# Attention probabilities read back through GpSimd's DMA queue, an activation table load tied to a later place, and extra TensorE products ahead of the first real ones

## The chip, the cores and the metric

The kernel runs on one core of a Trainium2 chip. The metric is the device time of one execution in microseconds (us). The kernel before takes 2250.06 us (median of three runs, 2249.04 to 2250.57). A profile of one execution shows what each engine did: TensorE (PE, with its weight loads as PEld), VectorE (DVE), ScalarE (ACT), GpSimd (POOL) and SyncE (SP), which issues most of the transfers between SBUF, the memory on the core, and DRAM.

## The reference

Four sequences of 512 tokens with 512 channels pass through two layers. Each layer has an attention-like part and a feed-forward part, each behind a gate made from a second input f:

```python
x = x + mamba2(bi_wkv(x, f, f, ...))          # layer 0, scan
x = x + moe(bi_wkv(x, f, f, ...))             # layer 0, 8 experts, top 2
x = x + grouped_attention(bi_wkv(x, f, f, ...))   # layer 1, 16 heads in 4 groups
x = x + silu_ffn(bi_wkv(x, f, f, ...))        # layer 1, 1408 wide
```

The gate runs two exponential averages over time, forward and backward, over `exp(k)*v` and `exp(k)`, and gives `sigmoid(r) * num / den`. Of the attention, these lines matter here:

```python
scores = einsum('bqgpd,bkgd->bgqpk', q, k) * SCALE
scores = where(causal, scores, -inf)
probs  = softmax(scores, axis=-1)
ctx    = einsum('bgqpk,bkgd->bqgpd', probs, v)
out    = einsum('bse,eh->bsh', ctx, w_dense)
```

## The kernel before, in words

Activations are held with channels on the 128 partitions and time along the free axis; weights stand still in TensorE's array and activations stream through it, 512 columns at a time. All products are in 32-bit floating point, except for the last stage, which splits its activations in two. The program is written as one stream. A planner that builds it sets the order of the instructions on each engine from the dependencies and from its own estimate of their costs. `tc.issue_after(i)` forces what is issued inside it to come behind `i` on the same engine; `after(engine)` does so for the last instruction that the engine has been given, and `Tables.use` ties a load of ScalarE's function table behind all activations that used the table before. Each engine carries out its instructions strictly in its own order, and a transfer queue sends off its transfers in order too: one that waits for data or for a free buffer holds those behind it.

**The opening (L943 to L1331).** The gate of sequence 0 is made in two pairs of channel blocks by `gate_pair` (L221): scans on VectorE, exponentials on ScalarE. L322 writes `den` times its reciprocal, L326 and L331 finish the gate, and L1311 multiplies it with the activated input into `first`, the input `h` of the scan stage. The weights `wxb` are loaded from L963 on. Eight PSUM banks (`ahead`, L1304) are taken in advance. `conv_products` (L1050, products at L1052) fills them with half of the sum after the first pair and the other half after the second; `conv_taps` (L1060, L1067) applies the four-tap convolution on VectorE. `time_steps` (L971, products at L977) needs a bank of the kind `tp`, two of which are among those eight, so it waits until the taps of one of them are done. `pump` fetches steps of the next gates' work, which VectorE does in between.

**Attention (L1568 to L1805).** There are 64 heads, in an outer order of group, sequence, and four heads within both. For a group and sequence `start_group` makes keys (`pk`, L1609) and values (`pv`, L1617). For a head `queries` makes `pq` (L1631) one head ahead, `scores` makes four query blocks of 128, 256, 384 and 512 keys (`psc`, L1653), masks them (L1656), takes the negated maximum (L1658), the exponential with its sum on ScalarE (L128, by way of L1663), divides by the sum (L1665), and turns blocks of 32x32 on VectorE into the SBUF tile `turned` (L1669), of which there are two. The other half of the transposition is done by memory: GpSimd issues four transfers that write `turned` to DRAM (L1677), and SP issues one that reads it back as `pT` (L1694, in `collect`), of which there are two buffers. `collect(1)` stands at the start of the next head's scores and leaves the youngest head in DRAM. `context` (L1719) multiplies `pT` with the values three heads later, and after each fourth head `dense` (L1734) applies the output weights and adds to the residual (L1742). The last two heads are transposed by TensorE (L1706). `nudge` (L1660) lets VectorE do a step of the gates of layer 1 between a maximum and the exponentials; those gates load `kt`, `ek` and `ekv` on SP's queue (L240, L247, L249). At the end of the stage `act.use(act.SILU)` (L1805) loads the table that the feed-forward stage needs.

Of the kernel before, what the change touches and what calls it, by code (L numbers as in the profile page):

```python
# [18 lines left out]
P = 128  # L19
B, T, C = 4, 512, 512  # L20
NC = C // P
# [62 lines left out]
def block_kernel(ctx: ExitStack, tc: tile.TileContext, a: dict, out: bass.AP):  # L84
    nc = tc.nc

    @contextmanager
    def after(*engines):

        with ExitStack() as es:  # L90
            for e in engines:
                last = next(
                    (i for i in reversed(nc.cur_bb.bb.instructions) if i.engine == e.engine), None
                )
                if last is not None:
                    es.enter_context(tc.issue_after(last))
            yield
# [35 lines left out]
    act = Tables()  # L133
# [32 lines left out]
    ident = const.tile([P, P], F32, name="ident")  # L166
# [51 lines left out]
    eks = [dr.tile([P, NC, T], F32, name=f"ek{b}") for b in range(B)]  # L218
    ekvs = [dr.tile([P, NC, T], F32, name=f"ekv{b}") for b in range(B)]

    def gate_pair(l, b, c0, dst=None, tiles=None):  # L221


        many = {"kt": 2, "ek": 2, "num": 2, "ekv": 1 if l < 2 else 2}
# [72 lines left out]
        den = tile_("den", 2)  # L297
# [14 lines left out]
        if tiles is not None or l >= 2:  # L312
            yield True

        r = tile_("rec", 2)
# [6 lines left out]
        nc.vector.scalar_tensor_tensor(  # L322
            flat(den), flat(den), DEN_MIN, flat(r), ALU.max, ALU.mult
        )
        yield False
        nc.vector.scalar_tensor_tensor(  # L326
            flat(num), flat(num), tf_out[:, b : b + 1], flat(r), ALU.mult, ALU.mult
# [573 lines left out]
    with ExitStack() as ph:  # L901
# [13 lines left out]
        first = even.tile([P, NC, T], F32, tag="h", name="h0_0")  # L915
# [9 lines left out]
        def lend_halves():  # L925

            left = []
            def take():
# [6 lines left out]
        lent = [  # L935
            {"f": lend("y", 3), "eu": lend("tmp", 2)},
            {
                "kt": lend("zs", 3), "ek": lend_halves(), "ekv": lend("xde", 2),
                "f": lend("xdt", 2), "eu": lend("bc", 4), "den": lend("st", 1, (P, DI)),
                "rec": lambda: lend("yT", 1, (P, NDI, P))().rearrange("p (i t) -> p i t", t=T),  # L940
            },
        ]
        pairs = [gate_pair(0, 0, c0, first, lent[c0 // 2]) for c0 in range(0, NC, 2)]  # L943
        for pair in pairs:
            for _ in range(6):
                for _ in step(pair):
# [8 lines left out]
        wxb = wx.tile([P, NC, NX], F32, name="wxb")  # L955
# [339 lines left out]
        def rounds(n):  # L1295
# [8 lines left out]
        ahead = [(m % NCV, ps_) for m, ps_ in zip(  # L1304
            range(NDI, NDI + 8), [ps_mm] * 4 + [ps_acc] * 2 + [ps_tp] * 2)]
        ahead = [(m, ps_("pc")) for m, ps_ in ahead]
        for c0, pair in zip(range(0, NC, 2), pairs):
            for _ in pair:
                pass
            for cc in range(c0, c0 + 2):  # L1310
                nc.vector.scalar_tensor_tensor(  # L1311
                    first[:, cc, :], turned[cc], 1.0, first[:, cc, :], ALU.add, ALU.mult
                )
            for m, pc in ahead:
                conv_products(w.h, m, pc, range(c0, c0 + 2))
# [202 lines left out]
    with tc.tile_pool(name="moe_w2", bufs=1, reuse_waits="tile") as wm:  # L1518
# [33 lines left out]
        n = len(nc.cur_bb.bb.instructions)  # L1552
# [15 lines left out]
    with att as ph:  # L1568
# [120 lines left out]
        def collect(rest=0):  # L1689

            while len(away) > rest:
                d = away.pop(0)
                back[id(d)] = pT = new_pT()
                nc.sync.dma_start(  # L1694
                    out=pT.rearrange("p r k j -> p (r k j)"), in_=d.rearrange("c i r s -> (c i) (r s)")
                )

        def context(u, prs):

# [46 lines left out]
        def settle():  # L1746

            old, done = held.pop(0)
            context(old, done)
            if len(old.ctxT) == HPG:  # L1750
                dense(old)

        weights, dense_w = {0: first_group}, {0: load_dense(0)}
        heads_ = [(g, b, i) for g in range(GROUPS) for b in range(B) for i in range(HPG)]
# [21 lines left out]
        for n, (g, b, i) in enumerate(heads_):  # L1776
            u, qT = ready
            if g == 0 and i == 0 and b + 1 < B:
                combine(b + 1, (0, 1))
                look_ahead(b + 1, (2, 3))  # L1780
            if g == 0 and i == 1 and b + 1 < B:
                combine(b + 1, (2, 3))
            if g == 0 and i == 3 and b + 2 < B:
                look_ahead(b + 2, (0, 1))
            if g == 2 and i == 0 and b < 3:
                to, name = ((ffg_d, "gateT"), (ffu_d, "upT"), (ffd_d, "downT"))[b]
                nc.sync.dma_start(out=to, in_=a[name])
            if g and b == 0 and i == 3:
                dense_w[g] = load_dense(g)
            if n + 1 < len(heads_):  # L1790
                ready = begin(n + 1)
            if g == 0 and i == 2 and b + 1 < B:
                act.use(act.EXP)
                hs[b + 1] = gated(2, b + 1, x[b + 1], gp, tag="h", name=f"h2_{b + 1}")
                act.use(act.LOG_EXP)
            prs = scores(u, i, qT)
            held.append((u, prs))
            if len(held) > 3:
                settle()
        while held:  # L1800
            settle()
        for _ in making:
            pass
        send()
        act.use(act.SILU)  # L1805


    LOW = 0xFFF
# [2 lines left out]
    with ExitStack() as ph:  # L1811
# [48 lines left out]
        for lo, hi in ((0, 4), (4, 8), (8, NFF)):  # L1860
            nc.sync.dma_start(
                out=wdn[:, lo:hi, :],
                in_=ffd_d[lo * P : hi * P, :].rearrange("(i p) m -> p i m", p=P),
            )

        for b in range(B):
            hd = []
            for i in range(NFF):
                cs = slice(i * P, (i + 1) * P)
# [38 lines left out]
        with tc.If(n_odd > 0):  # L1908
            with ExitStack() as gen:
                wl = gen.enter_context(tc.tile_pool(name="ff_gen", bufs=2, **right))  # L1910
                for b in range(B):
                    h = gated(3, b, x[b], gp, tag="h", name=f"h4_{b}")
                    hd = []
                    for i in range(NFF):
                        cs = slice(i * P, (i + 1) * P)
                        pv = []
                        for name in ("gateT", "upT"):
                            w = wl.tile([P, NC, P], F32, tag=name, name=name)
                            nc.sync.dma_start(
                                out=w, in_=a[name][:, cs].rearrange("(k p) m -> p k m", p=P)  # L1920
# [13 lines left out]
                    for m in range(NC):  # L1934
                        w = wl.tile([P, NFF, P], F32, tag="downT", name="downT")
                        nc.sync.dma_start(
                            out=w,
# [77 lines left out]
```

## Time and profile before

| what | us |
|---|---|
| median of three runs | 2250.06 |
| profiled execution, its own time | 2257.3 |
| its span, first to last instruction | 2255.4 |
| start of TensorE's first long work (L1052) | 42.02 |
| start of attention's keys (L1609) | 1129.81 |
| last dense products of attention begin (L1734) | 1995.81 |

The span is a little shorter than the profiled execution's own time, which includes what lies around it. How attention's TensorE work looks late in the stage, when no gates are made any more (start, duration, engine, line, operation, tiles, records; a product in 32-bit floating point leaves two records):

```profile
1949.51 3.60 PE L1631 MATMUL pq<-h,wq 128*128 128x512 f32 x8
1952.95 2.32 PE L1653 MATMUL psc<-kT,qT 128*128 128x128 f32 x8
1955.11 2.32 PE L1719 MATMUL pctx<-pT,v 128*128 128x512 f32 x8
1957.26 3.60 PE L1631 MATMUL pq<-h,wq 128*128 128x512 f32 x8
1960.70 2.32 PE L1653 MATMUL psc<-kT,qT 128*128 128x128 f32 x8
1962.86 2.32 PE L1719 MATMUL pctx<-pT,v 128*128 128x512 f32 x8
1965.01 13.90 PE L1734 MATMUL pd<-cx,wd 128*128 128x512 f32 x32
```

One head follows another without a gap: queries of the next head, scores of this one, context of the head three before. Starts show the pace better than durations, since the modelled ends overlap a little with the next start.

### The profile page before, as it was taken

The numbers are of one execution on the slowest core, as the hardware profiler recorded it, in microseconds if no ns is written. First come the engines' busy times: TensorE is split into PE (matmuls) and PEld (weight loads), VectorE is DVE, ScalarE is ACT, GpSimd is POOL, SyncE is SP. The second block draws the span as 40 slices with busy tenths as digits, with TensorE's granted clock in tenths as the row PEclk, the third lists the DMA queues.
The fourth block names the chain that finished last, engine by engine and source line by source line (L and its number), as shares of the span: only waits on it lengthen the run. The fifth ranks groups of instructions, "written<-read, shape, count | busy, mean of one in ns | idle before, by whom it ended". The sixth has DMA issues, their size and how long they took to land. (4 is left out here: it accounts for less than half of the span.)

```text
span 2255.4 us, 23842 instructions
## 1 busy us (share of the span) xinstructions
PE 2133.1 (95%) x7528; PEld 1227.2 (54%) x7528; DVE 1523.8 (68%) x3040; ACT 969.9 (43%) x1898; POOL 418.5 (19%) x558
## 2 busy tenths in 40 slices
PE   2879999999999999999989999999999999999998
PEld 1445565565665444444445555555555555568887
DVE  8697989989753566576577777577767765465332
ACT  4475676675842233333154433333334332243221
POOL 4023232322222111222211111111111111100000
PEclk9888999999999999999989999999999999999999
DMA  7542251342433457988576555455545464441100
GB/s 263 169 145 66 89 173 66 110 157 76 139 119 126 145 201 274 366 298 301 205 253 196 187 173 176 137 170 177 173 153 169 141 194 136 145 156 38 38 19 20
DMA packets 112454, 357.38 MB, mean 158 GB/s; under 512 B 14594, under 2 KB 23170, under 8 KB 102914
## 3 DMA queue, kind: packets, MB, share of 16 engines
q1 hardware_dynamic: 87584, 277.26, 36.3%
q0 software_dynamic: 22432, 74.34, 10.9%
q10 hardware_dynamic: 2304, 4.20, 0.5%
q8 instruction: 62, 1.02, 0.2%
q14 instruction: 72, 0.57, 0.1%
HBM read 337.91 MB, written 108.00 MB: 198 GB/s over the span
## 5 line engine op out<-in xcount | busy, mean ns | idle before, releaser
L1677 POOL DMA_DIRECT2D turned<-turned x248 | 135.2, 552 | 697.2 <-DVE turned L1669 393.7
L1631 PE MATMUL pq<-h,wq 128*128 128x512 f32 x512 | 233.2, 597 | 1.1 <-DVE h L404 0.8
L1734 PE MATMUL pd<-cx,wd 128*128 128x512 f32 x512 | 224.1, 594 | 3.1 <-ACT cx L1727 2.8
L128 ACT ACTIVATE pr<-psc,nmax 128x128 f32<-128x128 f32 (+3 forms) x256 | 134.6, 526 | 166.8 <-DVE nmax L1658 163.7
L1052 PE MATMUL pc<-h,wxb 128*128 128x512 f32 x320 | 150.9, 628 | 43.6 <-DVE h L1311 38.6
L1656 DVE TENSOR_TENSOR psc<-psc,mask 128x128 f32<-128x128 f32 x256 | 70.7, 284 | 144.3 <-PE psc L1653 144.1
L1653 PE MATMUL psc<-kT,qT 128*128 128x128 f32 (+3 forms) x512 | 155.7, 440 | 9.5 <-ACT pr L128 9.1
L1719 PE MATMUL pctx<-pT,v 128*128 128x512 f32 (+3 forms) x512 | 152.9, 438 | 9.4 <-DMA pT<-turned 9.1
L1734 PEld LDWEIGHTS pd<-cx,wd 128*128 128x128 f32 x512 | 95.5, 190 | 120.0 <-issue 107.9
L1631 PEld LDWEIGHTS pq<-h,wq 128*128 128x128 f32 x512 | 93.5, 192 | 97.2 <-issue 90.7
L1719 PEld LDWEIGHTS pctx<-pT,v 128*128 128x128 f32 x512 | 97.1, 191 | 90.0 <-issue 60.2
L845 PE MATMUL po<-w,yT 128*128 128x512 f32 x296 | 134.2, 593 | 0.9 <-DMA w<-in_w2x 0.7
L812 PE MATMUL pg<-w,hT 128*128 128x512 f32 x296 | 134.3, 594 | 0.0
L823 PE MATMUL pn<-w,hT 128*128 128x512 f32 x296 | 133.4, 593 | 0.5 <-DMA w<-in_w1x 0.5
L1052 PEld LDWEIGHTS pc<-h,wxb 128*128 128x128 f32 x320 | 62.5, 201 | 116.7 <-issue 74.4
L1742 DVE TENSOR_TENSOR xr<-xr,pd 128x512 f32<-128x512 f32 x64 | 43.6, 681 | 120.5 <-PE pd L1734 120.5
L1658 DVE TENSOR_REDUCE nmax<-psc 128x1 f32<-128x128 f32 (+3 forms) x256 | 122.4, 482 | 2.0
L1669 DVE STREAM_TRANSPOSE turned<-pr 128x128 f32<-128x128 f32 x248 | 120.5, 498 | 1.8
L1653 PEld LDWEIGHTS psc<-kT,qT 128*128 128x128 f32 x512 | 85.1, 191 | 66.8 <-issue 26.1
L1271 PE MATMUL po<-wot,yT 128*128 128x512 f32 x256 | 115.0, 603 | 0.0
L1123 PE MATMUL pz<-wzt,h 128*128 128x512 f32 x256 | 114.6, 596 | 0.3 <-ACT st L1224 0.3
L1665 DVE TENSOR_SCALAR pr<-pr,rsum 128x128 f32<-128x128 f32 (+3 forms) x256 | 95.5, 374 | 1.7
(343 smaller groups left out, 4146.9 us busy)
## 6 DMA issues: line engine op xcount, KB each, us to landing
w<-in_w1x SPq DMA_DIRECT2D x76, 1024.0 KB
turned<-turned POOLq DMA_DIRECT2D x248, 208.0 KB, 4.0
pT<-turned SPq DMA_DIRECT2D x62, 832.0 KB
w<-in_w2x SPq DMA_DIRECT2D x38, 1024.0 KB
wb<-in_b1x SPq DMA_DIRECT2D x38, 512.0 KB
lm<-cs SPq DMA_DIRECT2D x32, 512.0 KB
kt<-in_fT SPq DMA_DIRECT2D x62, 256.0 KB
ek<-ek SPq DMA_DIRECT2D x62, 256.0 KB
```

Of the source, the lines that this page charges most:

```text
L128: nc.scalar.activation(*args, **kw)
L812: nc.tensor.matmul(pg, lhsT=hT[:, k, :], rhs=self.w1[s][0][:, k, :], start=(k == 0), stop=(k == NC - 1))
L823: nc.tensor.matmul(pn, lhsT=hT[:, k, :], rhs=self.w1[s][1][:, k, :], start=(k == 0), stop=(k == NC - 1))
L845: nc.tensor.matmul(po, lhsT=yT[:, j, :], rhs=self.w2[s][:, j, :], start=(j == 0), stop=(j == NI - 1))
L1052: nc.tensor.matmul(pc, lhsT=wxb[:, k, m * P : (m + 1) * P], rhs=h[:, k, :], start=(k == 0), stop=(k == NC - 1),)
L1631: nc.tensor.matmul(pq, lhsT=u.wq[:, k, i * KVC : (i + 1) * KVC], rhs=u.h[:, k, :], start=(k == 0), stop=(k == NC - 1),)
L1653: nc.tensor.matmul(psc[:, :n], lhsT=qT[:, qi * P : n], rhs=u.kT[:, :n], start=True, stop=True)
L1658: nc.vector.tensor_reduce(nmax, psc[:, :n], AX.X, ALU.max, negate=True)
L1669: nc.vector.transpose(blocks[:, :, 3 * qi : 4 * qi + 1, :].rearrange("p c k j -> p k c j"), pr)
L1677: nc.gpsimd.dma_start(out=d[:, :, r].rearrange("c i s -> i c s"), in_=blocks[r * SQ : (r + 1) * SQ].rearrange("i c k j -> i c (k j)"),)
L1719: nc.tensor.matmul(pctx[:, kj * P :].rearrange("p (q r j) -> p q r j", r=QUAD, j=SQ), lhsT=u.v[:, kj, :], rhs=pT[:, :, 4 * kj : 10 + kj : ...
L1734: nc.tensor.matmul(po, lhsT=dense_w[u.g][:, i, m * P : (m + 1) * P], rhs=u.ctxT[i], start=(i == 0), stop=(i == HPG - 1),)
```

## The change

Three things are changed.

- In the opening, after the eight banks are taken, 16 products with 64 output columns each are put ahead of the real ones (`halves`): the identity's column halves times the first two blocks of `wxb`, eight with 512 moving columns and eight with 128. They write the two halves of the first bank. When L322 of the first pair has written `den`, `note` calls `warm`, which issues five products of the whole identity with `den` into the same bank. The first real product of that bank starts a new sum and overwrites what they left.
- `collect` issues the read of `pT` on GpSimd's queue, behind the last instruction that GpSimd has been given.
- The last table load of attention is tied behind the last ScalarE instruction that has been written down at the end of the last but one head's turn of the loop.

```diff
-    def gate_pair(l, b, c0, dst=None, tiles=None):
+    def gate_pair(l, b, c0, dst=None, tiles=None, note=None):
...
             flat(den), flat(den), DEN_MIN, flat(r), ALU.max, ALU.mult
         )
+        if note is not None:
+            note(den)
         yield False
...
-        pairs = [gate_pair(0, 0, c0, first, lent[c0 // 2]) for c0 in range(0, NC, 2)]
+        pairs = [
+            gate_pair(0, 0, c0, first, lent[c0 // 2], None if c0 else (lambda t: warm(t)))
+            for c0 in range(0, NC, 2)
+        ]
...
         ahead = [(m, ps_("pc")) for m, ps_ in ahead]
+
+        def halves(n):
+            bank = ahead[0][1]
+            for i in range(2):
+                cs = slice(i * 64, i * 64 + 64)
+                nc.tensor.matmul(
+                    bank[cs, :n], lhsT=ident[:, cs], rhs=wxb[:, i, :n], start=True, stop=True
+                )
+
+        def warm(t):
+            bank = ahead[0][1]
+            for i in range(5):
+                nc.tensor.matmul(bank, lhsT=ident, rhs=t[:, i % 2, :], start=True, stop=True)
+
+        for n in (512, 512, 512, 512, P, P, P, P):
+            halves(n)
         for c0, pair in zip(range(0, NC, 2), pairs):
...
                 back[id(d)] = pT = new_pT()
-                nc.sync.dma_start(
-                    out=pT.rearrange("p r k j -> p (r k j)"), in_=d.rearrange("c i r s -> (c i) (r s)")
-                )
+                with after(nc.gpsimd):
+                    nc.gpsimd.dma_start(
+                        out=pT.rearrange("p r k j -> p (r k j)"),
+                        in_=d.rearrange("c i r s -> (c i) (r s)"),
+                    )
...
             held.append((u, prs))
             if len(held) > 3:
                 settle()
+            if n == len(heads_) - 2:
+                last_row_over = [
+                    i for i in nc.cur_bb.bb.instructions if i.engine == nc.scalar.engine
+                ][-1]
         while held:
...
-        act.use(act.SILU)
+        with tc.issue_after(last_row_over):
+            act.use(act.SILU)
```

The changed code is longer, so its lines have other numbers: L1052 becomes L1057, L977 becomes L982, L1653 becomes L1674, L1694 becomes L1716 and L1719 becomes L1742.

## Prediction

> **What bounds the kernel now.** First the page's busy row, the clock row and the list of who waited for whom on TensorE.
>
> ```profile
> PE 2133.1 (95%) x7528; PEld 1227.2 (54%) x7528; DVE 1523.8 (68%) x3040; ACT 969.9 (43%) x1898; POOL 418.5 (19%) x558
> ...
> PEclk9888999999999999999989999999999999999999
> ```
>
> ```profile
> PE pc L1052 <- DVE h L1311: 38.6, 1, 38.6
> PE psc L1653 <- ACT pr L128: 9.1, 10, 1.9
> PE pctx L1719 <- DMA pT<-turned: 9.1, 4, 3.2
> ```
>
> TensorE is the bound: 2255.4 - 2133.1 = 122 us are not matmul, 38.6 of them one wait at the start. The clock is below full almost only in the first tenth. The third wait is the one that the change aims at. Next the opening in order of time (start, us, engine, line, records; a product of f32 leaves two records), the vector engine's product that the new warm-up reads, and the clock by stretches (third value).
>
> ```profile
> 42.02 3.78 PE L1052 MATMUL pc<-h,wxb 128*128 128x512 f32 x4 [38.58 <-DVE h L1311]
> 46.56 10.89 PE L1052 MATMUL pc<-h,wxb 128*128 128x512 f32 x25
> 79.59 6.68 PE L977 MATMUL pdt<-wxb,h 128*128 128x16 f32 x32 [2.83 <-DVE xc L1067]
> 86.11 3.76 PE L1052 MATMUL pc<-h,wxb 128*128 128x512 f32 x4
> 176.07 4.25 PE L977 MATMUL pdt<-wxb,h 128*128 128x16 f32 x32
> 33.64 1.22 DVE L322 SCALAR_TENSOR_TENSOR den<-den,rec 128x1024 f32<-128x1024 f32 x1
> ```
>
> ```profile
> 80.00:84.00 4.00, 4.00 (x21) 0.50 0.26 68
> 84.00:90.00 6.00, 6.00 (x16) 0.50 0.00 0
> ```
>
> The first four records take 0.95 us each, later ones 10.89 / 25 = 0.44: half speed at first. A 2.83 us gap then puts the clock back to 0.50 for ten microseconds; the same 32 records of L977 take 6.68 there and 4.25 later.
>
> Last, one pT stall, with the Sync and GpSimd queues around it.
>
> ```profile
> 1425.78 2.32 PE L1653 MATMUL psc<-kT,qT 128*128 128x128 f32 x8
> 1431.32 4.09 PE L1719 MATMUL pctx<-pT,v 128*128 128x512 f32 x8 [3.22 <-DMA pT<-turned]
> 1422.59 0.33 SPq L240 DMA_DIRECT2D kt<-in_fT  x1
> 1423.14 0.83 SPq L1694 DMA_DIRECT2D pT<-turned  x1
> 1411.82 2.17 POOL L1677 DMA_DIRECT2D turned<-turned  x4 [23.50 <-DVE psc L1656]
> ```
>
> And of the tile that GpSimd writes out: issues (ns, least, median, most) and the time to landing.
>
> ```profile
> L1677 POOL DMA_DIRECT2D turned<-turned x248: 550/550/677, 1158.2 to 1962.1; - x124
> DMA to landing us min/median/max: 2.7/4.0/8.2
> ```
>
> The head's probabilities went out at 1411.8 to 1414.0 and were in DRAM some 4.0 us later, at 1418. Their read stood on SP behind a kt load, which waits for a gate buffer (SP waits 254.6 us in total for L278), and left at 1423.1. So the cause is the queue's order, not the transfer.
>
> **The change part by part.** *Read-back.* 62 reads leave SP (0.32 us each there, which nobody waited for) and join GpSimd's queue, each behind the next head's four writes. At about 0.55 us each (the writes' median) that is 34 us on an engine that is 19% busy. A read waits there for its own writes to land and for a pT buffer, so for the context of two heads before it; behind it stand the next head's writes, whose transposes end some 9 us after their scores begin (1402.53 to 1411.82), later than that context, so nobody is held. The order of the built code moves too: SP loses only these reads, but TensorE now does, for each group of four heads, two contexts one step later (scores, queries, scores, then the context, then keys and values, then the second). Time left for the read, in the unit above: scores of the group's last head begin at 1402.53 and its writes end at 1414.0; the previous head's read leaves then, at about 1414.6, and lands by 1422.8 at the slowest landing, 8.2. Its context comes, by the new order, after four scores, two contexts and three queries: 4 x 2.16 + 2 x 2.15 + 3 x 3.44 = 23.3 us after 1402.53, so at 1425.8. Spare: 3.0 us at the worst landing, 7.2 at the median. The second late context has 7.0 even at the worst: it follows another context, keys, values and queries (2.15 + 3.43 + 3.57 + 3.44 = 12.6), while its read leaves 8.6 later (writes at 1420.45). So the four waits go: -9.1. The 4.09 of the stalled context against 2.32 for an unstalled one is the clock falling after the wait: -1.8. Against it, the group's fourth scores come one context (2.15 us) sooner after the third, with VectorE 66 to 73% busy in the stretches from 1250 to 1750: the 9.1 us of waits for ACT's exponentials may shrink (the order mixes queries in between) or grow by up to 2.15 in each of 12 groups with gate work. Bounds -5 and +22; I take +2, near what such waits cost per group today (0.67 + 0.67 + 1.02 + 0.16 + 1.02 = 3.5 us after 1275, in the order of time). Sum -8.9.
>
> *Table load.* One load (1.28 us) stays one; it now follows the context copy. TensorE shows no wait for it. 0, covered by the 13.7 us dense product; uncovered 1.28.
>
> *Opening.* 16 column-half products and five of den. The first need wxb, issued from 18.75: two loads of 648 KB at 338 GB/s from 21 end near 25. Eight of 512 columns cost two records each, 0.43 warm, 0.86 cold; the eight of 128 by the 128-column rows 0.21 to 0.43. If the clock rises 3.8 us after the start, as it does after 42.02 (to about 45.8), they end at 25 + 3.8 + 5.8 x 0.86 + 8 x 0.21 = 35.5; cold throughout, at 25 + 13.8 + 3.4 = 42.2. The den products need L322, done at 34.9: 10 x 0.43 = 4.3, so 35.5 to 39.8, inside TensorE's 38.58 us idle. The 2.2 us to 42.02 is a gap shorter than the 2.83 that cost the clock. Gain: four records, 3.78 - 4 x 0.43 = -2.1. Behind it the built order moves three gate operations of VectorE (L278, L265, L280: 0.69 + 1.28 + 0.67 = 2.6 us) from ahead of the convolution's taps into the step-size chain. L977 starts some 3 us sooner; with no gap before it, 6.68 becomes 4.25 (-2.4), and one product instead of two behind it saves 3.76 / 2 = -1.9; the three operations give back +2.6. Together about -4.7 with the clock kept, about -2.3 without. As VectorE and TensorE are both nearly full from 110 on (23.2 and 21.0 of 25 us), I let -3 through. Bounds: -7 (all of it) and +7 (cold throughout: the den products end at 42.2 + 8.6 = 50.8, less the 2.1).
>
> Sum: -8.9 - 3 + 0 = -11.9 on the profiled execution's 2257.3 (span 2255.4), that is 2245.4. That execution is 7.2 above the median of the runs, so the forecast is 2250.1 - 11.9 = **2238**.
>
> **The rivals.**
> *Scores take over the wait (chance 0.15).* The earlier fourth scores stall 12 times by some 0.75 us, 9 us in place of the 8.9 saved; only the opening's 3 us stay: 2247. For: five of the ten exponential waits stand there today. Against: the queries mixed in, and no such wait after 1765, where gates are done.
> *The opening does not warm (0.16).* The column halves use half the array; if that does not count as activity, the den products run cold from 42.2 or the clock has fallen again by 42. Then the opening gives between 0 and +7, middle +3.5, and the read-back stays: 2250 - 8.9 + 3.5 = 2245; at 0, 2241. The Trainium skill, TensorE: Matmul & The Clock Gate, Part 1, says an idle window of about 3.4 us lowers the clock and that windows run freely. The 2.83 us gap here already cost it, so 2.2 is near the edge.
> *The read on GpSimd's queue is late (0.13, the slower side).* Each read waits behind the next head's writes. From a landing of 8.2 + 3.0 = 11.2 us on, the first late context of each group stalls. At 13 us that is 1.8 in each of 15 groups, 27 us, plus clock falls of 1.8 in some five: 36 less the 3 of the opening: 2283; at 11.8 us, 9 us in all, so 2256. Against: no landing on that queue exceeded 8.2. For: a read is 832 KB where a write is 208. Under the same VectorE work the 248 write issues never took over 677 ns. The Trainium skill, SBUF — State Buffer, the "DVE blocks DMA" trap, says otherwise: VectorE locks GpSimd out of the ports through which it writes descriptors, and 620 ns alone became about 3100. By that rule, an estimate, five issues per head would take 12.4 us more, the read in the unit above would land some 5 us late and each group stall by that, 78 us in all; the trace disagrees with it so far, and I give it 0.02 of the 0.13.
> *The change does not shift the reads (0.04):* if they leave no sooner than today, the pT waits stay: 2247.
>
> **How the numbers follow.** Forecast 0.52 at 2238, own range 2230 to 2244. Faster by over 0.2% (about what this measurement tells from none; below 2245.6): 0.52 + most of the second rival 0.12 + 0.05 of the first and last = 0.69. Within 0.2%: 0.17. Slower: 0.13 of the late read, 0.01 of a cold opening: 0.14. The range 2229 to 2252 holds all but the late read and the far ends.
>
> **What would show it.** Right: no wait of L1742 (the context's new number) for pT; the read's landing on POOL under 11 us; the first records of L1057 at 0.43; the clock at full from 42 to 90 and L982 near 4.25; TensorE's psc waits for pr near 9. Wrong: psc waits of 18 or more, a wait of pctx on pT once per group, the den products still running at 42, or L1057 starting later than 42.0.

## The result, and the profile after

The changed kernel takes 2242.4 us (median of 22 runs, 2236.9 to 2248.6) where the kernel before took 2249.0 beside it (22 runs, 2240.8 to 2258.0). The ratio is 0.9969, 95% interval 0.9958 to 0.998: 6.6 us or 0.3% faster. Measured again later beside other kernels it gave 0.9947 (0.9924 to 0.997). The forecast was 2238, 11.9 us faster.

The two profiled executions, 2257.3 and 2242.7 us, differ by 14.6, more than twice what the medians do. So times are read from them stage by stage below.

First the busy row and the clock row of the page of the changed kernel (shares of the span; tenths of full clock in 40 slices), then the waits of TensorE (total us, times, longest).

```profile
PE 2135.2 (95%) x7570; PEld 1224.9 (55%) x7570; DVE 1526.2 (68%) x3039; ACT 968.9 (43%) x1899; POOL 455.8 (20%) x620
...
PEclk9989999999999999999989999999999999999999
```

```profile
PE pc L1317 <- DMA wxb<-in_in_projT: 20.9, 1, 20.9
PE psc L1674 <- ACT pr L128: 14.4, 15, 5.8
PE pk L1630 <- ACT pr L128: 2.1, 4, 0.9
```

The wait of 38.6 us at the start is broken up and the wait of the context for `pT` (9.1) is gone. But the scores' waits for exponentials went from 9.1 to 14.4, and one of them alone is 5.8, longer than any in attention before. Of GpSimd's added 37.3 us (418.5 to 455.8) the 62 reads, at 557 ns each, are 34.5.

The opening in order of time (start, us, engine, line, records):

```profile
24.25 8.20 PE L1317 MATMUL pc<-wxb,ident 128*64 128x512 f32 x32 [20.87 <-DMA wxb<-in_in_projT]
34.99 4.56 PE L1324 MATMUL pc<-den,ident 128*128 128x512 f32 x10 [2.54 <-DVE den L322]
42.10 33.74 PE L1057 MATMUL pc<-h,wxb 128*128 128x512 f32 x78 [2.56 <-DVE h L1332]
76.92 3.72 PE L982 MATMUL pdt<-wxb,h 128*128 128x16 f32 x32 [1.07 <-DVE xc L1072]
80.48 1.33 PE L1057 MATMUL pc<-h,wxb 128*128 128x512 f32 x2
94.49 0.49 PE L1144 MATMUL pp<-xc,xc 128*128 128x128 f32 x2 [2.03 <-ACT xc L128]
```

and two stretches of it (the value behind the five engines' columns is the granted clock, here 0.65 and 0.95; before, it was 0.50 in both):

```profile
80.00:84.00 4.00, 4.00 (x11) 1.94 (x11) 2.86 (x7) 0.92 (x2) 0.00 (x0) 0.65 0.03 13
84.00:90.00 6.00, 6.00 (x14) 2.42 (x12) 5.83 (x18) 0.00 (x0) 0.00 (x0) 0.95 0.15 44
```

The step-size product (L982) starts 2.7 us sooner than before (79.59), takes 3.72 in place of 6.68, and one product instead of two stands behind it. The first gram product (L1144, `pp`, the matrix product of the scan stage's first chunk with itself) starts at 94.49; before, it started at 100.55. It is the mark by which openings are compared below.

The moved reads: duration of an issue on GpSimd (ns: least, median, most), and from issue to landing (us).

```profile
L1716 POOL DMA_DIRECT2D pT<-turned x62: 553/557/582, 1160.9 to 1955.6; - x62
...
DMA to landing us min/median/max: 4.5/7.3/9.2
```

And the new wait, on TensorE, on ScalarE, and on the Sync queue:

```profile
1177.38 0.81 PE L1674 MATMUL psc<-kT,qT 128*128 128x384 f32 x2
1184.03 2.07 PE L1674 MATMUL psc<-kT,qT 128*128 128x512 f32 x2 [5.84 <-ACT pr L128]
```

```profile
1181.93 1.38 ACT L1515 ACTIVATE rr<-rr,g 128x512 f32<-128x512 f32 x2 [5.46 <-DMA rr<-rows_o]
1183.22 0.67 ACT L128 ACTIVATE pr<-psc,nmax 128x512 f32<-128x512 f32 x1
```

```profile
1168.24 7.53 SPq L1508 DMA_DIRECT2D rr<-rows_o  x4
```

In the first group of heads the rows that the experts left in DRAM (`rr`) are scaled on ScalarE and added to `x` (`add_results`, L1515). The planner's new order puts the scaling of two row tiles ahead of a head's last exponential. Their loads left between 1168 and 1176, each with a buffer to wait for, and ScalarE stands idle for 5.46 us until they are there; the exponential, and TensorE's next scores behind it, stand with it.

Of the signs that the prediction named, those of the read-back hold (no wait for `pT`, landings under 11 us), and the first records of L1057 take 0.43 us after a first one of 0.53. Two miss: the clock is at half from 81.2 to 84.6, and the scores' waits are 14.4, between the 9 of "right" and the 18 of "wrong". One sign of "wrong" came by a hair: L1057 starts at 42.10, not by 42.0.

### The profile page after: what moved, and what is told of

Same layout as the page of the kernel before. It is cut to its first block, busy times and chain, and to the rows that moved or that the text cites. A ratio compares the mean times of both kernels' runs of the same rounds, so it can differ in the third digit from the quotient of the medians.

```text
span 2241.0 us, 23830 instructions
## 1 busy us (share of the span) xinstructions
PE 2135.2 (95%) x7570; PEld 1224.9 (55%) x7570; DVE 1526.2 (68%) x3039; ACT 968.9 (43%) x1899; POOL 455.8 (20%) x620
## 4 chain that ended last, share of the span: by engine, by line
PE 40%; DVE 8%; ACT 1%; DMA 1%; issue 0%; DVEq 0%; ACTq 0%
PE pd L1757 10%; PE pq L1652 6%; PE pctx L1742 4%; PE psc L1674 4%; PE pk L1630 3%; PE pv L1638 3%; PE pfo L1873 2%; PE pfo L1872 2%; PE pfg L1872 2%; PE pfg L1873 2%; PE pfu L1872 2%; PE pfu L1873 2%; DVE nmax L1679 1%; DVE turned L1690 1%; DVE pr L1686 1%; DVE psc L1677 1%
## 5 line engine op out<-in xcount | busy, mean ns | idle before, releaser
L1674 PE MATMUL psc<-kT,qT 128*128 128x128 f32 (+3 forms) x512 | 160.0, 442 | 15.5 <-ACT pr L128 14.4
L1057 PE MATMUL pc<-h,wxb 128*128 128x512 f32 x320 | 145.6, 610 | 6.6 <-DVE h L406 4.0
L1742 PE MATMUL pctx<-pT,v 128*128 128x512 f32 (+3 forms) x512 | 148.4, 433 | 0.0
L1742 PEld LDWEIGHTS pctx<-pT,v 128*128 128x128 f32 x512 | 96.7, 190 | 76.2 <-issue 50.5
L1674 PEld LDWEIGHTS psc<-kT,qT 128*128 128x128 f32 x512 | 84.9, 191 | 74.2 <-ACT pr L128 29.7
L1057 PEld LDWEIGHTS pc<-h,wxb 128*128 128x128 f32 x320 | 60.8, 195 | 78.0 <-issue 71.5
```

The source lines that it names most:

```text
L1057: nc.tensor.matmul(pc, lhsT=wxb[:, k, m * P : (m + 1) * P], rhs=h[:, k, :], start=(k == 0), stop=(k == NC - 1),)
L1674: nc.tensor.matmul(psc[:, :n], lhsT=qT[:, qi * P : n], rhs=u.kT[:, :n], start=True, stop=True)
L1742: nc.tensor.matmul(pctx[:, kj * P :].rearrange("p (q r j) -> p q r j", r=QUAD, j=SQ), lhsT=u.v[:, kj, :], rhs=pT[:, :, 4 * kj : 10 + kj : ...
```

## The experiments

Two stretches carry the comparison, because whole runs scatter by some 10 us either way: the start of the first gram product (opening), and the time from the first keys product of attention (L1609, later L1630) to the last instruction (attention and what follows). What lies between, the scan and expert stages, took 1015 to 1030 us over the 14 profiles, and the differences there go with the clock: of the time lost to half clock in it (half of what the clock records spend at 0.5) the shortest two had 20.5 and 21.4 us, the longest two 35.1 and 35.5.

| kernel | ratio to before, 95% | gram start | keys to end |
|---|---|---|---|
| before | 1 | 100.5 | 1125.6 |
| after | 0.9969 (0.9958 to 0.998) | 94.5 | 1120.8 |
| after, again (e17_after_again) | 0.9947 (0.9924 to 0.997) | 96.8 | 1117.3 |
| opening alone (e1_open) | 0.9991 (0.9972 to 1.0011) | 97.2 | 1123.6 |
| read-back alone, no tie (e2_read) | 1.0000 (0.9983 to 1.0018) | 99.1 | 1128.4 |
| no den products (e4_halves) | 0.9963 (0.9944 to 0.9983) | 100.1 | 1121.7 |
| no halves (e5_den) | 0.9956 (0.994 to 0.9972) | 96.9 | 1120.2 |
| full columns (e9_full) | 1.0068 (1.0041 to 1.0094) | 118.0 | 1119.4 |
| more halves, no den (e7_long_halves) | 0.9966 (0.9948 to 0.9983) | 97.0 | 1121.4 |
| scaling tied (e14_scale_tied) | 0.9952 (0.9932 to 0.9972) | 96.8 | 1119.4 |
| kt loads on ScalarE (e13_kt_act) | one run | 100.9 | 1122.3 |
| first group on Sync (e11_sp_g0) | 0.9916 (0.9896 to 0.9935) | 97.2 | 1110.6 |
| the same, more halves, no den (e12_both) | 0.9925 (0.9908 to 0.9942) | 94.5 | 1110.0 |
| the same, opening as before (e16_no_open) | 0.9918 (0.9889 to 0.9947) | 100.6 | 1111.8 |

**The opening alone.** The reads back on Sync, the table load untied, as before:

```diff
-                with after(nc.gpsimd):
-                    nc.gpsimd.dma_start(
+                nc.sync.dma_start(
...
-        with tc.issue_after(last_row_over):
-            act.use(act.SILU)
+        act.use(act.SILU)
```

> The opening alone: the warm-up products stay, the probabilities are read back on the Sync queue and the last table load is untied, as before. Theory A (the forecast's two parts are independent and the opening is worth more than the 3 us let through): the first product of a gram (line 1144 in after) starts at 94.5 as in after, 6.1 us ahead of before, the scan stage hands most of it on, the four waits for pT of 9.1 us in all are there again, and the ratio to before is 0.997 to 0.9985 (-3.5 to -6.5 us). Theory B (VectorE, nearly full in the next stage, eats the lead): the same 94.5, but the first keys product starts less than 2 us earlier than in before and the ratio is 0.999 to 1.001.

The pT waits were there again (9.2 us, five times). The gram product started at 97.2, neither 94.5 nor 100.5, and the same program part behaved otherwise than in after:

```profile
24.29 6.66 PE L1317 MATMUL pc<-wxb,ident 128*64 128x512 f32 x32 [20.97 <-DMA wxb<-in_in_projT]
34.95 7.40 PE L1324 MATMUL pc<-den,ident 128*128 128x512 f32 x10 [4.00 <-DVE den L322]
```

The clock rose at 27.1 instead of 30.0, the half columns were done 1.5 us earlier, the rest until den became 4.0 us instead of 2.54, and the clock fell in it: ten den records took 7.40 in place of 4.56. An early rise opens the gap that undoes it: in the four executions of this program part in which the clock rose at 27.1 to 28.0, the rest was 3.60 to 4.00 us and the clock fell in it. The ratio does not decide between the theories: the interval holds -6 and +2 us. The first keys product came 17.2 us earlier than in before's profile, but 13.9 of that arose between the gram product and the keys, where the two differ by 14.6 in time lost to half clock.

**The read-back alone.** Before, with the reads on GpSimd, no warm-up, no tie:

> The read-back on the GpSimd queue alone: the opening as before and the last table load untied. Theory A (the queue's order was the cause of the pT waits, and the moved order costs one new stall of 5.8 us on ScalarE's scaling of the expert rows): no wait of the context for pT, the 5.8 us wait of the scores for the exponential near the end of the first group, waits for exponentials of 13 to 16 us in all, and a ratio of 0.997 to 0.9995 (-1 to -6 us). Theory B (the whole gain of the change is the opening): waits for exponentials and the clock give all of the 9.1 us back, ratio 0.9995 to 1.0015.

The waits were as A said (none for pT, exponentials 13.1 in all, longest 6.0), the ratio as B said, and for a reason in neither theory, on ScalarE and TensorE at the end of attention:

```profile
1955.20 1.28 ACT L115 ACT_TABLE_LOAD   x1
1956.50 1.15 ACT L128 ACTIVATE th<-xr 128x512 f32<-128x512 f32 x2
...
1962.06 0.56 ACT L1729 COPY cx<-pctx 128x512 f32<-128x512 f32 x1
```

```profile
1962.68 9.83 PE L1736 MATMUL pd<-cx,wd 128*128 128x512 f32 x19 [5.67 <-ACT cx L1729]
```

Without the tie the planner puts the last table load, and with it the next gate's activations and casts, ahead of the copy of a finished context, and the dense product waits 5.67 us for it. From the end of one dense product to the end of the next took 53.6 us there against 46.2 in after, where ScalarE's order is

```profile
1955.60 0.58 ACT L1750 COPY cx<-pctx 128x512 f32<-128x512 f32 x1
1956.19 1.28 ACT L115 ACT_TABLE_LOAD   x1
```

So beside the moved reads the tie is worth 7.4 us. What it would do alone, in the kernel before, was not run.

**Without the den products.** After with `note` left out, so that TensorE rests from the last half column to the first real product:

```diff
-            gate_pair(0, 0, c0, first, lent[c0 // 2], None if c0 else (lambda t: warm(t)))
+            gate_pair(0, 0, c0, first, lent[c0 // 2])
```

> After without the ten records that read den, so that TensorE rests from the last half-column product at 32.5 to the first real one at 42.1. Theory A (a rest of 9.6 us drops the clock): the first real records take 0.95 us again, the clock row shows about half speed after the rest, the 32 records of the step-size product take about 6.7, and the first gram product starts within 1.5 us of before's 100.55; the ratio to before is that of the read-back alone (0.997 to 0.9995). Theory B (the clock, once raised, holds through such a rest): records of 0.43 from 42 on, the gram product at about 95 to 97 and a ratio as after's, 0.996 to 0.998.

A, as to the opening:

```profile
42.44 35.66 PE L1054 MATMUL pc<-h,wxb 128*128 128x512 f32 x76 [8.89 <-DVE h L1329]
80.56 5.48 PE L979 MATMUL pdt<-wxb,h 128*128 128x16 f32 x32 [2.45 <-DVE xc L1069]
```

The clock, up at 31.0, fell at 37.8 in the rest and rose again at 48.1; the gram product started at 100.1, as if nothing had been put ahead (the step-size records took 5.48, under the 6.7 that A expected). Yet the ratio is after's, 0.9963, within B's range and under A's. The kernel has the reads on GpSimd and the tie. In the traces its instructions stand in the order of the read-back alone on all four engines, but for the sixteen extra products and the work around the last table load: what the read-back alone lacked was the tie. This kernel, with a cold opening, is thus not told apart from after.

**Full columns instead of halves.**

```diff
-                    bank[cs, :n], lhsT=ident[:, cs], rhs=wxb[:, i, :n], start=True, stop=True
+                    bank[:, :n], lhsT=ident, rhs=wxb[:, i, :n], start=True, stop=True
```

> After with the column halves replaced by products over all 128 columns (same count, same reads, same den products); by the built order VectorE then keeps before's order of the three gate operations ahead of the step-size chain. Theory A (the lead at the gram product is part clock, part order): the clock is up as in after, the first real records take 0.43, but the three operations of 2.6 us stand ahead of the chain again, so the step-size product starts at about its old distance, near 78, the gram product starts near 96.5 to 98 (3 to 4 us ahead of before instead of 6.1), and the ratio is 0.997 to 0.999. Theory B (the lead is all clock): the gram product at 94 to 95 and a ratio as after's, 0.996 to 0.998. If half columns do not count as activity, the clock in the rest is higher here than in after and the last warm-up product before the den ones ends sooner than 32.5.

Neither. The clock rose at 28.5, but the gram product started at 118.0 and the kernel lost 0.7%. VectorE and TensorE:

```profile
83.47 0.43 DVE L243 TENSOR_SCALAR ek<-kt 128x512 f32<-128x512 f32 x1 [17.11 <-DMA kt<-in_fT]
83.82 15.30 DVE L1072 SCALAR_TENSOR_TENSOR xc<-pc,cols,xc 128x509 f32<-128x509 f32 x23
```

```profile
84.71 8.01 PE L1057 MATMUL pc<-h,wxb 128*128 128x512 f32 x12 [13.22 <-DVE xc L1072]
```

The planner put a step of the next gate (L243) ahead of the convolution's taps, and its load was 17 us away. The width of the extra products cost nothing in itself (the first real product still started at 42.05); it changed the planner's order on another engine, and the gram product came 20 us later than A expected.

**Only the den products, and only more halves.** In the first the sixteen half-column products are left out (`for n in ...: halves(n)`), in the second the den products are left out and the halves are `(512,) * 8 + (P,) * 4`.

> After without the sixteen column-half products: TensorE rests until den is there at 34.9, then runs ten records that start at half clock. Theory A (some 7 us of den products are work enough to raise the clock and the last 1 to 2 us to the first real product do not drop it): the den products take 6 to 8.6 us, the first real records near 42 to 43.5 take 0.43 to 0.5 on the whole, and with VectorE's order nearly after's the first gram product starts at 94 to 97.5; ratio 0.996 to 0.998. Theory B (the clock needs the work from 24 on): real records of 0.95 for the first 4 to 7 us, the clock down again before 90, gram product at 98 to 101, ratio 0.997 to 0.9995.

> After with more column halves (eight times 512 columns and four times 128) in place of the den products, so that TensorE has no rest between 24 and the first real product; VectorE's built order is exactly after's. They take some 16 to 19 us and end at 40 to 43. Theory A (the rests of 2.5 to 4 us around the den products are what drops the clock in some executions, as in the opening-alone kernel, whose products ended at 30.95): clock at full from at most 32 to 75, first gram product at 94 to 95.5, or up to 1 us later if the halves run past 42; ratio 0.9955 to 0.9975. Theory B (half columns do not keep the clock up as long as full ones): a half-clock stretch between 33 and 45 and the gram product at 96 to 98.

The den products alone did what was wanted of both, as A said: they ran from 35.04 to 41.4, the clock rose at 38.6 and stayed until 79.6, gram at 96.9; the ratio, 0.9956, is a little under A's range. The longer halves took 11.65 us, not 16 to 19, and ended at 35.9; in the rest of 6.47 us after them the clock dropped, to half from 40.5 to 47.3, and the gram product still started at 97.0. So neither theory on the second was put to the test it was meant for. But it shows something else: its first real records ran at half clock until 47.3, no less than before's (until 45.8), and still the gram product came 3.5 us sooner. In the other parts the two kernels are after, except that with the den products alone VectorE takes a few operations of the next gate in another order in the opening.

**Reads of the first group on Sync.** All later groups on GpSimd, the rest as after:

```diff
-            away.append(d)
+            away.append((d, u.g))
...
-                with after(nc.gpsimd):
-                    nc.gpsimd.dma_start(
+                with ExitStack() as order:
+                    if g:
+                        order.enter_context(after(nc.gpsimd))
+                    (nc.gpsimd if g else nc.sync).dma_start(
```

> After, but the first group of heads reads its probabilities back on the Sync queue as before (there the built order of TensorE is before's again, and no pT wait fell in that group), all later groups on the GpSimd queue. Theory A (the new 5.8 us wait comes from the order that the read-back on GpSimd leads to in the first group: ScalarE's scaling of the expert rows stands ahead of an exponential before its rows are loaded): the wait is gone, waits of the scores for exponentials are 7 to 10 us in all instead of 14.4, the stretch from the first keys product to the end of the last dense product takes 866 to 871 us instead of 874.4, and the ratio is 0.9935 to 0.996. Theory B (the wait is the price of the later contexts and comes back elsewhere): 873 to 876 us, ratio 0.996 to 0.998.

A, and more than expected: 0.9916, 2229.9 us. First key product to last dense product took 864.5 us, against 875.0 in after and 879.9 before. The waits in attention:

```profile
PE psc L1674 <- ACT pr L128: 8.8, 11, 1.9
...
PE pctx L1744 <- DMA pT<-turned: 1.7, 1, 1.7
```

The 5.8 us wait is gone, and the pT waits are 1.7 in place of 9.1. The one that is left is for the last read of the first group, which is still on Sync. Against what the expectation says, before has a wait there too: its four waits are for the reads of heads 15, 19, 23 and 31 (counted from 0, the first group being heads 0 to 15), 1.7 us of them for head 15. So each read that left Sync lost its wait, and the one that stayed kept it, here and in the two kernels built on this one (1.7 us each). TensorE's pauses from the first keys product to the last dense product are 15.1 us (before 24.6, after 20.6), the time lost to half clock 5.1 (7.5 and 9.6).

**The same with more halves and no den products.**

> The longer column halves without den products and the first group's reads on the Sync queue together. If both theories A hold (no rest of TensorE before the first real product; no scaling ahead of its rows), the first gram product starts at 94 to 95.5, the stretch from the first keys product to the end of the last dense product takes 866 to 871 us, and the ratio is 0.993 to 0.9955, 1 to 7 us under after. If the opening's lead is lost in the scan stage, the ratio is that of the first group's reads alone, 0.9945 to 0.997.

The gram product came as expected, but not by the reason given: the halves left a rest of 7.30 us, and the clock was at half from 38.4 to 45.2. It then held until 93.0, through the step-size product, and the gram product started at 94.5. So the rest before the first real product did not decide the mark; the clock at the step-size product and just behind it did. The two executions with 94.5 lost 0.8 and 1.7 us to half clock between 76 and the gram product, the six others with after's order or nearly (96.8 to 97.2) lost 3.4 to 5.1. Keys to the last dense product took 863.9, under the expected range. The ratio, 0.9925, is not under the 0.9916 of the kernel above, so the 2.7 us that this one is ahead at the gram product do not show at the end.

**The kt loads off the Sync queue.** Before, with the reads left where they were:

```diff
-            nc.sync.dma_start(out=kt[i], in_=a["fT"][cc * P : (cc + 1) * P, b, :])
+            (nc.scalar if l > 1 else nc.sync).dma_start(
+                out=kt[i], in_=a["fT"][cc * P : (cc + 1) * P, b, :]
+            )
```

> Before, with the gates' loads of kt for the last two layers issued on ScalarE's queue instead of the Sync queue; the reads of pT stay on Sync, and the built order of TensorE keeps its contexts where before has them. Theory A (a pT read is late because it stands behind a kt load that waits for a gate buffer): the waits of the context for pT fall from 9.1 us to under 2.5, although the reads are on the old queue; ScalarE, which now holds those waits, makes the scores wait longer for exponentials (over 15 us). Theory B (the reads are late for another reason, the transfer or the pT buffers): waits for pT of 7 to 11 us remain.

Between the two: 6.1 us in two waits instead of 9.1 in four. What stood ahead of the two that were left, on Sync, GpSimd and TensorE:

```profile
1358.56 0.32 SPq L251 DMA_DIRECT2D ekv<-ekv  x1
1359.11 1.27 SPq L1696 DMA_DIRECT2D pT<-turned  x1
```

```profile
1349.49 2.18 POOL L1679 DMA_DIRECT2D turned<-turned  x4 [21.60 <-DVE psc L1658]
```

```profile
1368.53 3.30 PE L1721 MATMUL pctx<-pT,v 128*128 128x512 f32 x8 [2.77 <-DMA pT<-turned]
```

The head was written out by 1351.7 and, with the 4.0 us of the prediction, in DRAM at about 1355.7; its read left at 1359.1, right behind another load of the gate, `ekv`, on which Sync had waited 13.7 us. The other wait has the same picture. The cause is any gate load that waits for a buffer, not kt's alone. This is a single execution, and the planner moved a few of TensorE's instructions by a step, so the 6.1 is no exact measure. The scores' waits for exponentials did not grow (9.1), against what A expected.

**The scaling of the rows tied.** After, with

```diff
-                combine(b + 1, (2, 3))
+                with after(nc.scalar):
+                    combine(b + 1, (2, 3))
```

> After, with one tie added: in the first group the scaling and adding of an item's second pair of expert-row tiles is put behind the ScalarE work already issued, so that it no longer stands ahead of the last exponential of a head. Reads all on the GpSimd queue. Theory A (that order alone makes the 5.8 us wait): the wait falls under 2 us, waits for exponentials are 9 to 12 us in all, the stretch from the first keys product to the end is 1112 to 1117 us (after and its like 1119 to 1122), ratio 0.994 to 0.9965. Theory B (the rows come late in any order and the wait moves to the next exponentials or to the transposes of the rows): the stretch stays at 1118 to 1122, ratio 0.996 to 0.998.

The order did make that wait: it fell from 5.84 to 0.71, and the waits for exponentials are 10.0, as A said. But B holds for the time: 1119.4, between the 1120.8 and 1117.3 of the two profiles of after. (The ratio, 0.9952, lies in A's range, but so does the 0.9947 of after beside it.) The waits in attention:

```profile
PE psc L1674 <- ACT pr L128: 10.0, 16, 1.3
PE pcb L1521 <- DVE rr L1516: 7.2, 6, 2.2
```

The transposes of the scaled rows (L1521) wait instead, 7.2 us against 3.2 in after: the two tiles are now scaled at 1200.2, some 16 us after their loads have left, and one transpose waits 2.17 us for them. So it was not that the rows come late in any order, as B had it; the tie only traded one badly placed instruction for another. The runs settle that what is done in the first group costs the 9 us between this kernel and the one with that group on Sync: counted from the first keys product, the fifth dense product ends at 324.0 in the latter, 332.7 here and 333.9 in after, so 8.7 and 9.9 us later; at the sixteenth and last one the distances are 9.3 and 10.5, little more. That group's queue and its order change together, so order alone is not isolated, but no wait for `pT` stands on the other side. The runs do not settle the 9 us term by term.

**The opening as before, beside the first group on Sync; after once more.**

> The read-back as in the kernel with the first group on Sync, the last table load tied, and the opening as before (no extra products). Theory A (read-back and opening add up): the stretch from the first keys product to the end is 1109 to 1112 us as with the opening, the first gram product starts at 99 to 100.6, and the ratio is 0.9925 to 0.995, 1.5 to 4 us above the two kernels with a warm opening (0.9916 and 0.9925). Theory B (the opening's lead is lost in the scan stage): ratio 0.9915 to 0.9925, no difference.

> The changed kernel itself, for a second profile of its opening and for its ratio beside the others. Theory A (the clock's windows run freely, so the warm-up's effect differs between executions of one program): the gram product starts anywhere from 94.4 to 97.3, the stretch from the first keys product to the end is 1119 to 1122 us, ratio 0.9955 to 0.998. Theory B (the opening of a program repeats): 94.5 again to 0.3 us.

The first has keys to end at 1111.8, so the read-back is independent of the opening, as A said; its ratio, 0.9918, is B's number, though the interval of 0.6% does not exclude A. The second gave A in the opening: 96.8 for the program that gave 94.5, with a rest of 3.60 us before den and the clock down from 34.9 to 38.3. Its 1117.3 and its 0.9947 are below what was expected.

## Why the prediction was right, and where its size was off

*Bounds and cause.* Right: the pT waits came from the queue's order. They went when the reads left Sync; two of four went when only kt's loads did, with TensorE's contexts nearly where before has them; and with the first group's reads left on Sync, that group's one wait stayed and the others went. In the kernels with reads on GpSimd the contexts come a step later as well; only the kernel with kt's loads moved keeps these two causes apart, and it was profiled once.

*Time left for the read.* Right. Forecast was 23.3 us from the scores to the context, so 11.2 from the read's issue at the tightest; in after the least distance from a read's issue to its context is 11.7, the next ones 12.1 to 12.8. The slowest landing was 9.2 rather than 8.2, and nobody waited. The rival that the read on GpSimd is late did not come: its issues took 553 to 582 ns, the writes no more than before. The "DVE blocks DMA" trap of the Trainium skill (SBUF — State Buffer) did not show here either, with VectorE 68% busy. The page ties it to VectorE operations in a 2-port perf mode; no run here shows whether there were any.

*Read-back, -8.9.* This is the term that was mis-sized. Mean of six profiles with all reads on GpSimd and the tie: 1120.1 us from keys to end, against 1124.6 for two with the reads on Sync: -4.5. Two opposite parts are in it. The three kernels with only the first group on Sync take 1110.8 on average: the later groups gave -13.8, more than the whole term, and the first group took back 9.3. The step that failed is "I take +2, near what such waits cost per group today". The 3.5 us that it rests on are all such waits after 1275 together, five of them, not the cost per group; in that stretch they did not grow (3.5 us in before, 2.6 in after). But most of the first group (the first sixteen heads), where the expert rows are added as well, lies ahead of 1275 and has no price of its own in the sum, and there the change cost 9.3: TensorE's pauses are 5.0 us longer on average and the time lost to half clock is 3.8 more. The wait of 5.84 is only the most visible of it, for the tie that removed it gained nothing. This is, in another place, what the first rival feared, that the scores take over the wait. The -1.8 for the clock came: the 1.7 us lost to half clock behind the stalled context of 3.2 us are in both profiles with the reads on Sync and in none of the six. What the six lose more than those two is nearly all in the first four heads. For the two profiled executions, pT (-9.1), copied contexts (L1734, -2.8), exponentials (+5.3), keys (+2.1) and half clock (7.5 to 9.6, +2.1) add up to -2.4, where the stretch shows -4.8; about 2 us of it have no wait to their name.

*Table load, 0.* Right for the change as a whole, wrong in its reason and in its "uncovered 1.28": without the tie the moved reads make the planner put the load and 5 us of other work ahead of a context's copy, and it costs 7.4. The reads alone gave 1.0000. That the sum could leave this out was luck of the prediction: the tie, to which it gave no worth, is what keeps the read-back's gain.

*Opening, -3 let through.* In the right place. Over eight profiles with VectorE's order as in after (or nearly) the gram product starts at 96.36 on average, over five with before's order at 100.25: -3.9, between -3 and -6. The reason is less sure. The five also have a cold clock at the first real product, and six of the eight a warm one; but the other two, the kernels with more halves, were cold there until 47.3 and 45.2 and lie among the eight, with 97.0 and 94.5. So the order that the extra products brought about on VectorE, and the clock at the step-size product, seem to weigh more than the warm start that the products were meant for; the term "four records" of -2.1 does not show, for the step-size product began at 77.2 and 78.4 in those two and at 76.9 to 77.6 in the six. No run has the warm start with before's order. What of the lead reaches the end is still open: from gram product to keys the same profiles take 1021.1 and 1022.4 on average, with a spread of 15. With the time lost to half clock taken off they take 995.2 and 993.5, so by an estimate from these two means some 1.7 of the 3.9 are given back on the way. In the medians nothing of the lead is to be seen: the kernels with and without the extra products (0.9916 and 0.9925 against 0.9918) are not told apart.

*The rival that the opening does not warm.* Half true. It warms, but the prediction's times for it, 35.5 for the end of the halves and 2.2 us for the last rest, assumed one course, and there are several. The Trainium skill, TensorE: Matmul & The Clock Gate, Part 1, says that the windows run freely and that the same kernel can see different numbers of cold products; the traces agree, with a rise at 27.1, 27.4, 27.8, 28.0, 30.0 and 31.0 for the same sixteen halves.

*The sum.* The measured read-back is -4.5; with all of the opening's -3.9 it would be -8.4. The two measurements, -6.6 and -10.8, do not say which. So the forecast's size, -11.9, is too large by about half in the term that carries it, and that 2242.4 still lies in its range of 2230 to 2244 is in part luck: two errors of the read-back, -13.8 where -8.9 stood and +9.3 where nothing stood, partly cancel.

## What to carry to other kernels

Where a planner orders the work, an edit that moves a transfer is also an edit of every engine's order: look in the built order for what was moved ahead of what in each stage that the transfer serves, above all the stage with the most neighbours, before pricing the wait that it removes. A gain can be lost in one place of the new order; undoing the edit only there (here the first of four groups) gave 0.9916 in place of 0.9969 and 0.9947. Keep transfers that somebody waits for off a queue whose other transfers wait for buffers.

## What the hardware showed that was not expected

A rest of 2.52 us before the first real product dropped the clock in one kernel (full columns, half speed from 42.2 to 45.6), while two rests of 2.54 and 2.56 in after did not; all seven rests of 3.60 to 8.89 us did. Nor does the clock need a rest to fall: in the step-size product, 32 records of 16 columns over 3.6 to 4.1 us with none ahead of them, it fell at 81.5 after longer halves, and in the same place with the first group on Sync it held until 93.0. Over the 14 profiles these half-clock stretches make up most of the difference between executions: from gram product to keys the times spread from 1015 to 1030 us, and with the time lost to half clock taken off only from 991.9 to 996.6.
